# An attention layer and a triangle layer on one core: y turned by VectorE for the last batch, put-off pieces at fixed groups, bounds taken batch by batch

## The chip, the core and the metric

The kernel runs on one core of a Trainium2 chip. A core has five engines, each with an instruction queue of its own that is worked off in order: TensorE (PE in the profile; its weight loads are PEld), VectorE (DVE), ScalarE (ACT), GpSimd (POOL) and SyncE (SP), which here only starts DMAs. Engines wait for one another through semaphores. The metric is the device time of one execution in microseconds; lower is better.

## The reference

The input x is 4 batches of 64 x 64 positions with 256 channels, so 4096 tokens per batch, in float32. Two layers follow one another.

Layer 0 is self-attention over the 4096 tokens of a batch, with 32 channels for queries and keys and 128 for values:

```python
s = jnp.einsum('bqd,bkd->bqk', g, f)
beta = jax.nn.softmax(s, axis=-1)
o = jnp.einsum('bqk,bkd->bqd', beta, v)
o = o @ Wo + bo
return x + o.reshape(b, h, w, c)
```

Layer 1 takes its result y as a 64 x 64 map and does triangle attention with 8 heads of 32 channels, then a projection, a residual with y, a layer norm, a two-layer MLP and a second layer norm:

```python
att = jax.nn.softmax(scores, axis=2)
out = jnp.einsum('biljh,bilhd,bljhd->bijhd', att, v1, v2)
attn_out = out.reshape(B, N, N, E) @ Wo
h = _layer_norm(x_in + attn_out, ln_agg_g, ln_agg_b)
mlp = jax.nn.relu(h @ W1 + b1) @ W2 + b2
return _layer_norm(mlp + h, ln_out_g, ln_out_b)
```

## The kernel before

The whole order of instructions is written out by hand; nothing is reordered inside `tc.manual_schedule()`. `run` goes through the four batches, and for each through layer 0 (`layer0`) and layer 1 (`first_layer1` or `next_layer1`). At the end, `rest.alone` does what is left of batch 3's tokens.

**Layer 0** (lines 498 to 844). A batch has 8 blocks of 512 queries (`NQB`), and each block has 8 groups (k = 0 to 7) of four chunks of 128 keys: 64 groups, counted by g. In group g TensorE computes the scores of group g+1 (`score`, L552) and the products with the values of group g (`values`, L579), alternating. ScalarE takes the exponential of the scores in two halves into a tile `e` (L564, tag k8, two buffers); VectorE adds `e` to the running sum `esum` (L584, L586). In group 7 VectorE adds the four quarters and splits the sum into two parts, `part` (L589 to L596, tag hid, one buffer). The work on a finished block is spread over the groups of the next one by the list `parts`: `norm` (den on TensorE, L604; then the reciprocal, L608, and oT, L610, on VectorE) and `bounds` in group 0, `output` in group 1 (y on TensorE, L631, to which VectorE adds the bias and the input, L632; y is stored to DRAM from SP, L635), and the projections to q, k, v1 and v2 (L646, L678) in groups 2 to 7, each with a copy on ScalarE into a tile `st` (three buffers) and a store from SP.

**Layer 1** (lines 848 to 1039 and 1491 to 1610) has 32 steps of products on VectorE and GpSimd (`product`, L1007) and sums of them on TensorE (`accumulate`, L1017). Word lists (ORDER, ORDER_LAST) set the order of one period, which is two steps in batches 1 to 3. `store` writes the result to DRAM.

**Tokens** (class `Tokens`, line 1044): what comes after the triangle product, in 16 pieces of 256 tokens per batch, tt = 16 b + t. The pieces of a batch run beside the layers of the next one; those of batch 3 run beside its own layer 1 (48 and 49, in part) and in `alone`. For a piece, `load` fetches the triangle result A and the piece of y; `heads` (L1120) projects A and adds y in the same PSUM accumulation. y lies in DRAM with channels first, so it has to be turned, and this is done on TensorE by a matmul against the identity, two for each half of a piece (L1125). `stats` and `roots`/`polish` make the layer norm's factors; `affine_a` applies them; `turn`, `hidden`, `rectify` and `outputs` are the MLP.

For batches 0 and 1, the last layer norm is put off: the raw sums go to DRAM, and are taken up in layer 0 of batches 2 and 3, as 16 put-off pieces. One such piece has six steps: `recall` (a DMA of 512 KB from SP into a tile `hz`, tag R, three buffers), `settle` (three two-input operations and the statistics on VectorE, L1073 to L1075, L1136, L1137), `rooted` (two small operations on ScalarE), `polished` (four small ones on VectorE, L1175 to L1178), `scaled` (two on ScalarE, L1197) and `finish` (two on GpSimd, L1287 and L1288, and a store from SP). Lines 760 to 763 set when: piece i is recalled in group 3 i, and its steps follow 3, 4, 5, 6 and 7 groups later, whatever the place of that group in its block.

**The bounds.** The sums of all softmax rows are kept in one tile `dens` for all batches (L618, L932), and two reductions at the very end (L1635, L1636) take their least and greatest value; if one is out of bounds, the kernel runs again in a safe form. These lines lie outside the manual schedule, and the compiler has set the reductions between the last products of layer 1.

SP's queue holds nearly all loads and stores in order. A DMA whose data or buffer isn't ready holds up all that stand behind it.

Of the kernel before, what the change touches and what calls it, by code (L numbers as in the profile page):

```python
# [10 lines left out]
F32 = mybir.dt.float32  # L11
# [4 lines left out]
ALU = mybir.AluOpType  # L16
AX = mybir.AxisListType

P = 128
C = 256  # L20
# [54 lines left out]
def attention_then_triangle_kernel(  # L75
# [29 lines left out]
    def ctile(shape, name):  # L105
        return const.tile(shape, F32, tag=name, name=name)
# [97 lines left out]

    dens = ctile([P, NB, 256 + 16], "dens")

# [235 lines left out]
    class Late:  # L446
# [4 lines left out]

        def load(self, q):
            self.y = []
            for cc, tag in enumerate(("A", "yc")):
                t = work.tile([P, 512], F32, tag=tag, name="yb", bufs=1)
                nc.sync.dma_start(out=t, in_=self.io["y"][ts(cc, P), ts(q, 512)])
                self.y.append(t)
            self.used = 0
# [39 lines left out]
    def layer0(b, F, safe, rest, ahead):  # L498
# [6 lines left out]
        io["q"] = dram.tile([C, 2, N, 32], F32, tag="q", name="q")  # L505
        io["v2"] = dram.tile([N, C, N], F32, tag="v2", name="v2d")
        io["v1"] = dram.tile([T, C], F32, tag="v1", name="v1d")
        L = Layer1(b, io, safe)


# [103 lines left out]
        def bounds(qb):  # L614
            for j, (t, op) in enumerate(ends.pop(qb)):
                if not safe:
                    c0 = 256 + 2 * qb + j
                    nc.vector.tensor_reduce(dens[:, b, c0 : c0 + 1], t, AX.X, op)  # L618

# [4 lines left out]
        def output(qb):  # L626
            col = ts(qb, QB)
            o = oT.pop(qb)
            for cc in range(2):
                y_ps = pb("y")  # L630
                nc.tensor.matmul(y_ps, wo0_sb[:, 0, ts(cc, P)], o, start=True, stop=True)  # L631
                nc.vector.scalar_tensor_tensor(  # L632
                    y(qb, cc), y_ps, bo_sb[:, cc : cc + 1], yT[cc][:, col], ALU.add, ALU.add
                )
                nc.sync.dma_start(out=io["y"][ts(cc, P), col], in_=y(qb, cc))  # L635


        def staged(st):
# [89 lines left out]
        if late:  # L728
            parts[3] = [lambda qb: proj(qb, "k", 0)]
            parts[4] = [lambda qb: proj(qb, "v2", 0)]  # L730
            parts[5] = [proj1_half]
            parts[6] = [lambda qb: proj(qb, "q", 1)]
            parts[7] = [lambda qb: proj(qb, "k", 1)]
        last = NQB - 1
        for r in range(4):
            score(0, r)
        for g in range(8 * NQB):
            qb, k = divmod(g, 8)
            if b == 0 and not safe:
                for load in later[3 * g : 3 * g + 3]:  # L740
                    load()
                if g == 6:
                    fold_bias()
                if g == 20:
                    add_b2()
            if safe and k == 0 and qb + 1 < NQB:
                mx, todo = pieces(qb + 1)
                for qc, t in todo:
                    max_piece(qc, t, mx)
                row[qb + 1] = max_row(mx)  # L750
            values(g, g + 1 < 8 * NQB)

            if qb > 0 and not (qb == last and k >= 6 + late):
                for part in parts[k]:
                    part(qb - 1)
            if late and g % 2 == 0 and 0 <= g // 2 - 2 < ahead.n:
                ahead.bring(g // 2 - 2)
            if late and g % 2 == 1 and 0 <= g // 2 - 3 < ahead.n:
                ahead.turn(g // 2 - 3)
            if b > 1:  # L760
                for do, late in ((rest.finish, 7), (rest.scaled, 6), (rest.polished, 5), (rest.rooted, 4), (rest.settle, 3), (rest.recall, 0)):
                    if (g - late) % 3 == 0 and 0 <= g - late < 3 * NP:
                        do(NP * (b - 2) + (g - late) // 3)
            if qb == last and k == 3:
                L.fetch_v1(0)
                L.fetch_v1(1)
            if qb == last and k == 5:
                if b > 0:
                    rest.load(NP * (b - 1))
                L.fetch_qk(0, True)  # L770
# [18 lines left out]
        if old:  # L789
            rest.stats_a(t0)  # L790
            rest.roots(0, 2)
            rest.polish(0, 2, nc.gpsimd)
        bounds(last)
        proj(last, "v2", 0, None, stage[1][:, 0, :], nc.scalar)
        L.fetch_v2(0, 1)
        mps = {}
# [53 lines left out]
    class Layer1:  # L850
        def __init__(self, b, io, safe):
            self.b, self.io, self.safe = b, io, safe

            self.aT = dram.tile([C, 2, N // 2, N], F32, tag="aT", name="aT")
            io["a"] = self.aT
            self.S, self.v2, self.qk, self.v1, self.att, self.ao = {}, {}, {}, {}, {}, {}
            self.R, self.begun, self.acc, self.rec, self.e = {}, {}, {}, {}, {}

# [60 lines left out]
        def sums(self, step):  # L921
            pair, ig = divmod(step, NIG)
            rows = self.S[pair][:, ts(ig, IG), :]
            if self.safe:
                nmx = small.tile([P, IG], F32, tag="mxl", name="mxl")
                nc.vector.tensor_reduce(nmx, rows, AX.X, ALU.max, negate=True)
                den = small.tile([P, IG], F32, tag="den", name="den")
                for i in range(IG):
                    nc.scalar.activation(rows[:, i, :], rows[:, i, :], AF.Exp, bias=nmx[:, i : i + 1])
            else:  # L930
                den = dens[:, self.b, ts(step, IG)]
            nc.vector.tensor_reduce(den, rows, AX.X, ALU.add)  # L932
            rec = small.tile([P, IG], F32, tag="rd", name="rd")
            nc.vector.reciprocal(rec, den)  # L934
            self.rec[step] = (rows, rec)
# [105 lines left out]

    class Tokens:
        def __init__(self):
            self.ios = []
            self.A, self.htp = {}, {}
            self.h, self.hT, self.hT2, self.hid, self.z, self.zp, self.hps = {}, {}, {}, {}, {}, {}, {}
            self.mv = self.rs = None
            self.raw, self.both, self.settled = {}, {}, {}  # L1050
# [44 lines left out]
        def load(self, tt, far=False):  # L1095
            b, t = divmod(tt, NP)
            if b >= len(self.ios):
                return
            io = self.ios[b]
            if far:  # L1100

                tag = ("v2", "S", "qk")[t % 3]
                both = big.tile([P, 2, 2, 256], F32, tag=tag, name="A", bufs=4 if tag == "v2" else 2)
                A, yc = both[:, 0].rearrange("p c (i j) -> p c i j", j=N), both[:, 1]
            else:
                A = work.tile([P, 2, 4, N], F32, tag="A", name="A", bufs=1)
                yc = work.tile([P, 2, 256], F32, tag="yc", name="yc", bufs=1)
            for c in range(2):
                for o in range(2):
                    nc.sync.dma_start(out=A[:, c, o : 4 : 2, :], in_=io["a"][ts(c, P), o, ts(t, 2), :])  # L1110
            nc.sync.dma_start(out=yc, in_=io["y"][:, ts(t, 256)].rearrange("(c p) t -> p c t", p=P))
            self.A[tt] = A, yc

        def heads(self, tt, n, psum=pb, new=None):
            if n == 0 if new is None else new:
                self.hps[tt] = psum("hp").rearrange("p (n c) -> p n c", n=2)
            hp = self.hps[tt]
            A, yc = self.A[tt]
            for cc in range(2):
                nc.tensor.matmul(  # L1120
                    hp[:, n, :], A[:, cc, ts(n, 2), :].rearrange("p i j -> p (i j)"), wo1_sb[:, cc, :],
                    start=(cc == 0), stop=False,
                )
            for cc in range(2):
                nc.tensor.matmul(  # L1125
                    hp[:, n, ts(cc, P)], yc[:, cc, ts(n, P)], ident, start=False, stop=(cc == 1),
                    is_transpose=True,
                )


        def stats(self, src, k, ns=range(2)):
# [5 lines left out]
                nc.vector.bn_aggr(self.mv[:, k + n, :], st)  # L1137

        def stats_a(self, tt):
            self.stats(self.hps[tt], 0)  # L1140

        def stats_o(self, tt):
# [291 lines left out]
    def first_layer1(L, ahead, F):  # L1434
# [27 lines left out]
                ahead.load(s + 2)  # L1462

        for period in range(NSTEP // 4 + 3):
            for word, late in words_of(ORDER0):
                i, last = period - late, int(word[-1])
                if word[0:2] == "sp":
# [23 lines left out]
    def next_layer1(b, L, rest, ahead, F):  # L1491
# [32 lines left out]
        def of_piece(word, q):  # L1524
# [8 lines left out]
                        load(q + 1)  # L1533
            elif word == "sa" and first:
                moments(q - 1)
                if own:
                    rest.stats(rest.hps[tt], 0)
                else:
# [51 lines left out]
        step_word, scores, take_scores = step_words(L, fetched, was_stored, spread)  # L1590
        mps[1] = {}
        for period in range(NP + 4):
            for word, late in words_of(ORDER_LAST if own else ORDER):
                i = period - late
                if own and i == 0 and word in ("A05", "A04"):
# [35 lines left out]


    lim = small.tile([P, 2], F32, tag="lim", name="lim", bufs=1)
    flat = dens.rearrange("p b n -> p (b n)")
    nc.vector.tensor_reduce(lim[:, 0:1], flat, AX.X, ALU.min)  # L1635
    nc.vector.tensor_reduce(lim[:, 1:2], flat, AX.X, ALU.max)  # L1636
    nc.vector.tensor_scalar(lim[:, 0:1], lim[:, 0:1], 1e-25, None, ALU.is_ge)
    nc.vector.tensor_scalar(lim[:, 1:2], lim[:, 1:2], 1e25, None, ALU.is_le)
    cnt = pb("cnt")
# [39 lines left out]
```

## Time and profile before

| | |
|---|---|
| median of 3 runs | 3628.52 us (3628.36 to 3633.21) |
| the profiled execution | 3633.17 us, its span 3631.4 us |
| mean granted TensorE clock | 0.994 |
| TensorE busy | 3522.3 us, 97% |
| VectorE busy | 2823.5 us, 78% |
| ScalarE busy | 1923.8 us, 53% |
| GpSimd busy | 1779.2 us, 49% |
| layer 0 of batches 0 to 3, from its first to its last value matmul | 45 to 411, 874 to 1262, 1734 to 2124, 2597 to 2987 us |
| tail (`alone`), in steady pieces | about 3480 to 3610 us |

Times in the profile count from the span's start. A line of a timeline gives the start, the time from the start of the first to the end of the last instruction merged into it, the engine, the line in the kernel, the operation, the tile written and the tiles read, and in brackets the idle time before it with what ended it. Matmuls overlap, so the length of one is more than its share of the array's time; the distance of starts tells that. A list of groups gives for each kind of instruction its count, its busy time, the mean length in ns and the idle time before it. A list of waits gives who waited for whom: total, times, longest. A table of stretches gives for each engine the busy time, then the granted TensorE clock, the share of time that the DMA engines were busy, and GB/s.

### The profile page before, as it was taken

To read this page: it belongs to the slowest core of one execution; us is meant where nothing else is said; L and a number is where in the kernel's file an instruction comes from. 1 tells how busy PE (TensorE), PEld (TensorE's weight loads), DVE (VectorE), ACT (ScalarE), POOL (GpSimd) and SP (SyncE) were. 2 spreads that over 40 slices of the span, in tenths; PEclk is the share of its full clock that TensorE was granted. 3 is DMA by queue.
4 is the path that set the end of the run, shared out by engine and by line. 5 is a ranking of instruction groups with operands and counts; after the bars stand their busy time and mean duration, and the time that the engine had idled before them with its cause. 6 is when DMAs were issued, how large, how long until landed. Compare 5 with 4: busy or idle time off the path is not lost.

```text
span 3631.4 us, 58644 instructions
## 1 busy us (share of the span) xinstructions
PE 3522.3 (97%) x22282; PEld 1895.3 (52%) x22282; DVE 2823.5 (78%) x2558; ACT 1923.8 (53%) x4221; POOL 1779.2 (49%) x904
## 2 busy tenths in 40 slices
PE   9999999988999999999999999999899999999998
PEld 6555444434555555554455555554455555555477
DVE  4777499996555569999777549999877756999976
ACT  3444455544444366665444446666444436777655
POOL 5000099995000068889211018889611106999920
PEclk9999999999999999999999999999999999999999
DMA  9544555455111354425423254343622235441221
GB/s 174 135 131 127 136 151 137 122 134 136 47 52 52 82 145 108 101 68 107 110 91 95 67 146 109 89 104 76 132 87 95 80 93 134 92 96 46 68 68 55
DMA packets 492594, 370.15 MB, mean 102 GB/s; under 512 B 303184, under 2 KB 434000, under 8 KB 483472
## 3 DMA queue, kind: packets, MB, share of 16 engines
q1 hardware_dynamic: 443264, 339.36, 34.8%
q0 software_dynamic: 36160, 19.94, 5.3%
q10 hardware_dynamic: 12880, 7.01, 0.7%
q8 instruction: 178, 2.92, 0.4%
q14 instruction: 112, 0.92, 0.1%
HBM read 205.73 MB, written 160.43 MB: 101 GB/s over the span
## 4 chain that ended last, share of the span: by engine, by line
PE 67%; POOL 8%; DVE 6%; issue 4%; ACT 1%; DMA 1%; SPq 0%; ACTq 0%; POOLq 0%; DVEq 0%
PE o L579 16%; PE acc L1017 16%; POOL Rp L1007 7%; PE proj L646 6%; PE mp L1253 5%; PE zp L1273 5%; PE s L552 4%; PE sp L905 3%; PE hp L1120 3%; DVE R L1007 2%; PE v1p L678 2%; PE att L959 1%; PE y L631 1%; DVE rec L608 1%; PE htp L1220 1%
## 5 line engine op out<-in xcount | busy, mean ns | idle before, releaser
L1007 POOL TENSOR_TENSOR Rp<-attP,v 128x2048 f32<-128x2048 f32 x328 | 1491.4, 4579 | 409.7 <-ACT attP L967 367.0
L1007 DVE TENSOR_TENSOR R<-att,v 128x2048 f32<-128x2048 f32 x696 | 1546.1, 2279 | 68.6 <-PE acc L1017 49.9
L579 PE MATMUL o<-e,v 128*128 128x512 f32 x2048 | 1043.9, 593 | 0.0
L586 DVE TENSOR_TENSOR esum<-esum,e 128x2048 f32<-128x2048 f32 x224 | 518.8, 2316 | 398.4 <-ACT e L564 395.9
L564 ACT ACTIVATE e<-s 128x1024 f32<-128x1024 f32 x512 | 522.3, 1023 | 529.2 <-PE s L552 438.7
L552 PE MATMUL s<-gT,fT 128*128 128x512 f32 x1024 | 786.7, 770 | 8.7 <-ACT e L564 4.7
L1017 PE MATMUL acc<-R,wsel 128*32 128x512 f32 x5568 | 702.8, 599 | 26.5 <-DVE R L1007 19.6
L579 PEld LDWEIGHTS o<-e,v 128*128 128x128 f32 x2048 | 388.2, 190 | 276.8 <-issue 234.0
L1027 ACT COPY ao<-acc 128x1024 f32<-128x1024 f32 x256 | 256.4, 1013 | 290.4 <-PE acc L1017 205.8
L1017 PE MATMUL acc<-Rp,wsel 128*32 128x512 f32 x2624 | 344.3, 596 | 25.6 <-POOL Rp L1007 23.2
L1017 PEld LDWEIGHTS acc<-R,wsel 128*32 128x32 f32 x5568 | 155.5, 109 | 393.7 <-issue 273.9
L552 PEld LDWEIGHTS s<-gT,fT 128*128 128x128 f32 x1024 | 194.5, 190 | 244.7 <-issue 230.8
L1287 POOL TENSOR_TENSOR hz<-hz,log_bc 128x512 f32<-128x512 f32 x32 | 47.1, 1471 | 542.8 <-ACT hz L1197 474.4
L1181 POOL TENSOR_SCALAR nt<-mv 128x2 f32<-128x2 f32 (+1 forms) x49 | 9.4, 192 | 565.2 <-DVE mv L1137 560.1
L942 ACT ACTIVATE es<-S,rd 128x64 f32<-128x64 f32 x1024 | 258.3, 338 | 15.0 <-DVE rd L934 13.1
L1253 PE MATMUL mp<-hT,w 128*128 128x256 f32 x1024 | 244.4, 384 | 1.7 <-ACT hT L1225 1.7
L1273 PE MATMUL zp<-w,hid 128*128 128x256 f32 x1024 | 239.4, 384 | 0.8 <-ACT hid L1262 0.8
L1253 PEld LDWEIGHTS mp<-hT,w 128*128 128x128 f32 x1024 | 186.5, 190 | 53.0 <-ACT attP L967 12.6
L1273 PEld LDWEIGHTS zp<-w,hid 128*128 128x128 f32 x1024 | 188.0, 190 | 47.8 <-issue 14.7
L608 DVE RECIPROCAL rec<-den 128x512 f32<-128x512 f32 x32 | 107.4, 3357 | 109.7 <-PE den L604 104.4
L1017 PEld LDWEIGHTS acc<-Rp,wsel 128*32 128x32 f32 x2624 | 80.7, 110 | 214.1 <-issue 144.9
L915 ACT ACTIVATE S<-sp 128x512 f32<-128x512 f32 x128 | 131.6, 1094 | 78.0 <-PE sp L905 78.0
(192 smaller groups left out, 3688.4 us busy)
## 6 DMA issues: line engine op xcount, KB each, us to landing
v<-v2d SPq DMA_DIRECT2D x44, 512.0 KB
v1c<-v1d SPq DMA_DIRECT2D x128, 128.0 KB
aT<-ao SPq DMA_DIRECT2D x1024, 16.0 KB
A<-aT SPq DMA_DIRECT2D x256, 64.0 KB
hz<-raw SPq DMA_DIRECT2D x32, 512.0 KB
y<-yT SPq DMA_DIRECT2D x56, 256.0 KB
q<-st SPq DMA_DIRECT2D x56, 256.0 KB
k<-st SPq DMA_DIRECT2D x52, 256.0 KB
```

The lines of the kernel that those rows point to most:

```text
L552: nc.tensor.matmul(s_ps[r // 2][:, r % 2, :], fT[tt][:, ts(r * 4 + n, P)], gT[qb // 4][:, ts(qb % 4, QB)], start=True, stop=not safe,)
L564: nc.scalar.activation(e[g][:, 2 * j : 2 * j + 2, :], s_ps[j], AF.Exp)
L579: nc.tensor.matmul(o_ps[qb], F.v[tt][:, r * 4 + n, :], es[:, r, :], start=(k == 0 and r == 0), stop=(k == 7 and r == 3),)
L586: nc.vector.tensor_tensor(esum[qb], esum[qb], es, ALU.add)
L608: nc.vector.reciprocal(rec, den)
L646: nc.tensor.matmul(ps, w[:, cc, rows], y(qb, cc), start=(cc == 0), stop=(cc == 1))
L942: nc.scalar.mul(e[:, i, :], rows[:, i, :], rec[:, i : i + 1])
L1007: eng.tensor_tensor(R, src.unsqueeze(1).to_broadcast([P, D, N]), v2[h], ALU.mult)
L1017: nc.tensor.matmul(acc[32 * c : 32 * c + 32, n % 2, :], w[:, n, c, 16 * h : 16 * h + 32], R[:, ts(c, 8), :].rearrange("p d j -> p (d j)"), ...
L1027: nc.scalar.copy(self.ao[step][:, ts(np, 2)].rearrange("p k d j -> p k (d j)"), self.acc[step][np])
L1253: nc.tensor.matmul(self.mp[:, fc % 2, :], w1_sb[:, cc, ts(fc, P)], self.hT[tt][:, cc, :], start=(cc == 0), stop=(cc == 1),)
L1273: nc.tensor.matmul(zp[:, n, :], self.hid[tt][:, fc, ts(n, P)], w2_sb[:, fc, :], start=(fc == 0), stop=(fc == 3 and tt not in self.hT2),)
```

## The change

There are three parts.

1. For the last batch (`turned_ahead(b)`), y is turned by VectorE in layer 0: `turn_y` does eight 128 x 128 transposes (in blocks of 32 x 32) per block in group 5 of the next block, into a tile of tag hid, and stores it from SP with four DMAs to a new DRAM tensor `yt`, tokens first, in runs of 256 bytes. For the last block this is done after the loop, into a tile of tag k8, and the stores are issued in period 1 of layer 1 (`L.owed`). `heads` leaves out the turning matmuls for this batch; `load` fetches from `yt`, and `add_y` adds the piece to PSUM on VectorE, ahead of the statistics.
2. The put-off pieces no longer come every third group. Blocks 0 and 1 take up three pieces each, blocks 2 to 6 two each, and block 7 none. Piece t of a block is recalled in group t, settled in group 2 + t + t//2, and so on; none of the steps of a piece passes its block's group 7.
3. `dens` holds one batch. `limits(b - 1)` takes its least and greatest value in group 1 of the next batch's layer 0, and `limits(NB - 1)` at the end.

```diff
-    dens = ctile([P, NB, 256 + 16], "dens")
+    dens = ctile([P, 256 + 16], "dens")
+    lims = ctile([P, 2, NB], "lims")
+    def limits(b):
+        for j, op in enumerate((ALU.min, ALU.max)):
+            nc.vector.tensor_reduce(lims[:, j, b : b + 1], dens, AX.X, op)
...
+        def turn_y(qb, **where):
+            t = work.tile([P, 16, 2, 32], F32, name="yr", **where)
+            for cc in range(2):
+                rows = y(qb, cc).rearrange("p (k t) -> p k t", t=32)
+                for k in range(4):
+                    nc.vector.transpose(t[:, ts(k, 4), cc, :], rows[:, ts(k, 4), :])
+            def kept():
+                for r in range(4):
+                    nc.sync.dma_start(
+                        out=io["yt"][ts(qb, QB), ts(r, 64)].rearrange("(k t) c -> t k c", t=32),
+                        in_=t[ts(r, 32)].rearrange("t k h c -> t k (h c)"),
+                    )
+            return kept
...
+        if turned_ahead(b):
+            parts[5].append(lambda qb: turn_y(qb, tag="hid", bufs=1)())
...
-                for do, late in ((rest.finish, 7), (rest.scaled, 6), (rest.polished, 5), (rest.rooted, 4), (rest.settle, 3), (rest.recall, 0)):
-                    if (g - late) % 3 == 0 and 0 <= g - late < 3 * NP:
-                        do(NP * (b - 2) + (g - late) // 3)
+                first = 3 * qb if qb < 2 else 2 + 2 * qb
+                for t in range(3 if qb < 2 else 2 if qb < last else 0):
+                    for do, at in (
+                        (rest.recall, t), (rest.settle, 2 + t + t // 2), (rest.rooted, 3 + t + t // 2),
+                        (rest.polished, 4 + t + t // 2), (rest.scaled, 5 + t + t // 2), (rest.finish, 7),
+                    ):
+                        if k == min(at, 7):
+                            do(NP * (b - 2) + first + t)
+            if g == 1 and b > 0 and not safe:
+                limits(b - 1)
...
         bounds(last)
+        if turned_ahead(b):
+            L.owed = turn_y(last, tag="k8")
...
+    def turned_ahead(b):
+        return b == NB - 1
...
+            src = io["yt"][ts(t, 256)] if turned_ahead(b) else io["y"][:, ts(t, 256)]
+            nc.sync.dma_start(out=yt, in_=src.rearrange("(n p) c -> p n c", p=P))
...
-                    start=(cc == 0), stop=False,
-                )
-            for cc in range(2):
-                nc.tensor.matmul(
-                    hp[:, n, ts(cc, P)], yc[:, cc, ts(n, P)], ident, start=False, stop=(cc == 1),
-                    is_transpose=True,
-                )
+                    start=(cc == 0), stop=(cc == 1 and turned_ahead(tt // NP)),
+                )
+            if not turned_ahead(tt // NP):
+                for cc in range(2):
+                    nc.tensor.matmul(
+                        hp[:, n, ts(cc, P)], self.yt[tt][:, cc, ts(n, P)], ident, start=False, stop=(cc == 1),
+                        is_transpose=True,
+                    )
+
+        def add_y(self, tt):
+            hp, yt = self.hps[tt], self.yt.pop(tt)
+            if not turned_ahead(tt // NP):
+                return
+            for n in range(2):
+                own = hp[:, n, :].rearrange("p (h r c) -> p h r c", h=2, r=4)
+                nc.vector.tensor_tensor(own, own, yt[:, n, :].rearrange("p (r h c) -> p h r c", h=2, r=4), ALU.add)
...
         def stats_a(self, tt):
+            self.add_y(tt)
             self.stats(self.hps[tt], 0)
...
+            if period == 1:
+                L.owed()
...
-    flat = dens.rearrange("p b n -> p (b n)")
-    nc.vector.tensor_reduce(lim[:, 0:1], flat, AX.X, ALU.min)
-    nc.vector.tensor_reduce(lim[:, 1:2], flat, AX.X, ALU.max)
+    limits(NB - 1)
+    nc.vector.tensor_reduce(lim[:, 0:1], lims[:, 0], AX.X, ALU.min)
+    nc.vector.tensor_reduce(lim[:, 1:2], lims[:, 1], AX.X, ALU.max)
```

## The prediction

> **What bounds the kernel now.** I read the page's first part, then TensorE's list of waits batch by batch, then the timelines of the blocks in which a wait stands, then the groups of the operations that the change adds or removes.
>
> ```profile
> span 3631.4 us, 58644 instructions
> PE 3522.3 (97%) x22282; PEld 1895.3 (52%) x22282; DVE 2823.5 (78%) x2558; ACT 1923.8 (53%) x4221; POOL 1779.2 (49%) x904
> ```
>
> TensorE runs for 97% of the span, so time can only come from its waits or from work taken off it. Its waits in layer 0 of batch 2 (window 1733 to 2130):
>
> ```profile
> PE proj L646 <- DVE yT L632: 1.9, 2, 1.0
> PE y L631 <- DVE oT L610: 0.3, 1, 0.3
> ```
>
> Group starts on the timeline of TensorE show what these are: a block of eight groups takes 50.8 us, but 52.0 in blocks 3 and 6, where put-off piece work (settle) falls on group 0 behind the softmax division, and 51.6 in block 1. Over undisturbed blocks that is 1.2 + 1.2 + 0.8 = 3.2 us, in batches 2 and 3 alike: 6.4 us in all. Batch 1, without put-off pieces, has none of it.
>
> Block 0 of batch 2 on VectorE (start, length):
>
> ```profile
> 1748.47 2.29 DVE L586 TENSOR_TENSOR esum<-esum,e 128x2048 f32<-128x2048 f32 x1 [2.06 <-ACT e L564]
> 1750.68 0.69 DVE L1073 TENSOR_TENSOR hz<-hz,lag_bc 128x512 f32<-128x512 f32 x1
> ...
> 1753.94 2.26 DVE L586 TENSOR_TENSOR esum<-esum,e 128x2048 f32<-128x2048 f32 x1
> ...
> 1766.98 3.33 DVE L586 TENSOR_TENSOR esum<-esum,e 128x2048 f32<-128x2048 f32 x1
> 1770.35 2.18 DVE L589 TENSOR_TENSOR esum<-esum 128x1024 f32<-128x1024 f32 x1
> ```
>
> A settle takes 3.26 us (1750.68 to 1753.94). The last two lines are 1.0 and 0.9 us longer than usual (2.29, 1.23); POOL is then in a finish whose second operation is stretched from 1.28:
>
> ```profile
> 1768.24 3.20 POOL L1288 TENSOR_TENSOR hz<-hz,lob_bc 128x512 f32<-128x512 f32 x1
> ```
>
> So each collision of a finish with VectorE's two-input sums costs VectorE about 1 us. What a settle waits for, on the DMA queue and in the stretches (last two numbers: DMA share, GB/s):
>
> ```profile
> 1738.35 0.43 SPq L417 DMA_DIRECT2D yT<-ahx  x1
> 1738.87 1.89 SPq L1068 DMA_DIRECT2D hz<-raw  x3
> ```
> ```profile
> 1742.00:1746.00 4.00, 4.00 (x12) 2.00 (x11) 2.34 (x2) 1.78 (x2) 0.00 (x0) 1.00 1.05 444
> 1746.00:1748.00 2.00, 2.00 (x8) 1.04 (x6) 0.42 (x1) 0.85 (x2) 0.00 (x0) 1.00 0.88 369
> 1748.00:1750.00 2.00, 2.00 (x8) 1.13 (x6) 1.53 (x1) 0.85 (x2) 0.00 (x0) 1.00 1.02 416
> ```
>
> The three recalls stand behind 3 MB of v and yT. Adding up GB/s from 1738, 3.67 MB (v, yT, first recall) are through at 1748.3; with a lagging engine I take 1749.6. The same sum in batch 3 gives 2611.6.
>
> The groups of the turning:
>
> ```profile
> L1125 PE MATMUL hp<-ident,yc 128*128 128x128 f32 x200 | 38.2, 273 | 0.0
> L356 DVE STREAM_TRANSPOSE xr<-xr 128x128 f32<-128x128 f32 x192 | 48.6, 388 | 0.0
> L1343 DVE TENSOR_TENSOR z<-zp,z 128x256 f32<-128x256 f32 x2 | 0.8, 404 | 0.0
> L1635 DVE TENSOR_REDUCE lim<-dens 128x1 f32<-128x1088 f32 x1 | 1.3, 1271 | 0.0
> ```
>
> And one piece of the tail on TensorE, from one hp to the next:
>
> ```profile
> 3502.93 1.03 PE L1120 MATMUL hp<-wo,A 128*128 128x256 f32 x4
> 3503.80 0.38 PE L1125 MATMUL hp<-ident,A 128*128 128x128 f32 x2
> 3504.01 1.03 PE L1120 MATMUL hp<-wo,A 128*128 128x256 f32 x4
> 3504.88 0.38 PE L1125 MATMUL hp<-ident,A 128*128 128x128 f32 x2
> 3505.10 0.60 PE L1220 MATMUL htp<-ident,h 128*128 128x128 f32 x4
> ```
>
> Starts count here: two turning matmuls hold the array from 3503.80 to 3504.01, 0.21 us. Pieces follow each other every 9.51 us without a gap.
>
> **The change part by part.** All sums are differences against the profiled execution, which took 3633.17 us (span 3631.4), 4.65 us over the median of 3628.52; I apply them to the median.
>
> *Turning matmuls gone, sums added (tail).* Four per piece: 0.43 us, so TensorE needs 9.08 per piece. VectorE gets two 128x256 sums from PSUM, 0.42 each by L1343's row. Its loop per piece runs from the first hp statistics (3543.35) to the last small operation (3551.70): 8.35 us, with two waits of 0.60 for ScalarE in it; then 1.17 us idle until hp. With the sums it needs 9.2, more than TensorE's 9.08, so VectorE sets the pace: 0.31 saved over 11 steady pieces, -3.5 us. Ends: TensorE keeps the pace over 14 pieces, -6.0; a sum costs as much as the 128x512 one of L1145 (0.68), loop 9.7, +2. I take -3.5, since L1343 has the right width. Pieces 48 and 49 run beside layer 1, where VectorE is busy 95%: +0.3 (0 to +0.8).
>
> *turn_y.* Eight transposes of 0.388 per block, 3.1 us on VectorE in group 5, which lasts 7.8 us and in which VectorE otherwise has one 2.3 us esum: hidden by the projections of that group. In block 1 a settle and a polish stand there too, 9.6 us; the 1.8 left over is made up in group 6. For the last block it stands in an idle stretch of VectorE (2998.9 to 3019.7); its four stores are issued in period 1 of layer 1, behind SP's loads for the start, and the k8 buffer they read is next wanted by ao of step 1, a period of 27 us later: 0. Without this cover it would cost 3.1 a block. The four stores of a block (0.55 each on SP) come behind the q store (2723.68 in block 2 of batch 3), so until 2726; behind them SP has the k store of 2729.8 and, in block 7, the loads of A, needed at 2989.5 and now there some 2 us before: 0 (to +1). Their buffer is shared with part, written at 2731.2. The nearest row, the v2 store of half the bytes in 256-byte rows, issued at 2735.81, is through by 2739.2; twice that ends near 2730, and den needs part only near 2739. Cost 0. [...]
>
> *Fixed groups.* Gone: the settles of group 0, and block 1's old wait: -6.4. In blocks 2 to 6 settles fall in groups 2 and 3 (VectorE 5.8 us in groups of 6.1 and 7.8): no wait follows. In block 0 groups last 4.35 and now hold three settles. Batch 2, group 2 from 1744.0: esum(2) ends 1746.4, settle waits for the recall (queued behind it: esum(3), then ScalarE's exponentials, which need e's buffers, then TensorE). Then without a pause: settle 1752.9, esum(3) 1755.1, settle 1758.4, esum(4) 1760.6, polish 1761.3, esum(5) 1763.5, polish 1764.2, settle 1767.5, esum(6) 1769.7, esum(7) 1771.9, half sums and part 1775.2, polish 1775.9; with one collision for each of two finishes, 1777.9. Scaled for the third piece stands on ScalarE in group 7 behind that polish: 1779.0; the exponential behind it ends 1780.1, and the score matmul that needs its buffer was due at 1774.6. Wait: 5.5 us. In batch 3 the recall is 0.7 earlier relative to its group: 4.8. Together 10.3, so +3.9 net. Ends: no collision and no late recall, about 0; two collisions for each finish, 14.3, and 2 more if block 1's third piece does the same at its end (by the same walk its exponential has 0.2 us to spare). SP holds the third store of block 0 until that finish ends, with recall and the y stores behind it; they are needed two groups later.
>
> *The clock.* TensorE's granted clock was 0.50 for 3.4 us after idle gaps of 2.55 us (at 414) and 2.46 (at 1718), but stayed at 1.00 after 2.46 at 2580. The new wait falls in two pieces of about 2.5 us (before den and before the score): I take one drop in two batches, 3.4 us at half speed, +1.7 (0 to +6.8). [...]
>
> *Bounds by batch.* limits adds two reductions of 272 columns (0.4 each) at group 1, where VectorE idles 4.4 us: 0. At the end the two 1.27 us reductions (3449.7, 3451.3) stand between products, and TensorE then waits 1.34 for R; they shrink by 1.7 in all: -1.0 (-1.3 to 0).
>
> Sum: -3.5 + 0.3 + 3.9 + 1.7 - 1.0 = +1.4: 3629.9 us.
>
> **The rivals.** *Faster:* VectorE's backlog never reaches TensorE and TensorE keeps the tail's pace: -6.4 - 6.0 - 1.0 = -13.4, 3615. For it: in block 3 a finish collided in group 7 and block 4 shows no wait. Against: the settles alone are 9.8 us in six groups of 4.35 that already hold 2.2 each.
> *Slower:* the same backlog at its upper end, 16.3 us in both batches, with clock drops of 6.8 us: +9.9 + 6.8 - 3.5 - 0.7 = +12.5, 3641. It decides once wait and drops pass 18 us for both batches. For it: VectorE would have no idle time from 1749.6 on. Against: a finish cost 2 us only where sums followed one another closely.
> *part waits for the stores of turned y:* from 5.5 us of lateness on each us costs six blocks 1 us; 2 more make +12, 3642. Against: the v2 store's 3.4 us.
> *The tail gains nothing* because the sums bound it: 3633.4, still no change.
>
> **How the numbers follow.** Forecast 0.50, tail without gain 0.10, faster 0.15, backlog 0.20, stores 0.05. About 0.2% (7.3 us) is what a measurement can tell from no change: faster 0.15, same 0.60, slower 0.25. Most of the chance lies within; the forecast's own range is 3622 to 3636. Leaving out the outer halves of the rivals gives 3619 to 3641.
>
> **What would show it.** In layer 0 of batches 2 and 3, blocks 3 and 6 take 50.8 us and block 1 some 56; VectorE has no gap from the first settle to rec; exponentials wait for scaled. Tail pieces follow every 9.2 us, and the gap before the hp statistics is gone. No turning matmul reads the last batch's y. It is wrong if recalls land sooner, if POOL collides otherwise, or if a sum on PSUM in place costs more than 0.42.

## The result, and the profile after

The changed kernel takes 3636.01 us in the median of 20 runs (3630.58 to 3640.49), the kernel before 3632.49 us in 20 runs beside it (3624.61 to 3635.48). The ratio is 1.0014, with a 95% interval of 1.0008 to 1.0021: 2.9 to 7.6 us longer. That is clearly more than nothing, and its upper end lies at the prediction's bound for no change (0.2%, 7.3 us). The forecast of 3629.9 us was worked out on a median of three runs of before that lay 4 us lower; as a difference it was +1.4 us. The profiled execution of after took 3637.93 us, its span is 3636.1 us (before 3631.4).

The first part of the page, after:

```profile
span 3636.1 us, 58663 instructions
...
PE 3521.2 (97%) x22218; PEld 1888.1 (52%) x22218; DVE 2862.1 (79%) x2662; ACT 1922.6 (53%) x4221; POOL 1770.2 (49%) x904
```

The shares say nothing: 64 matmuls fewer, 104 VectorE instructions more. The difference is read by stages: layer 0 from the start of the first value matmul (L586) to the start of the last one and its step of 0.43 us, and the tail from the last hp of layer 1's rhythm (at 3458.65 before and 3467.26 after) to the end. All are worked out from starts in the traces:

```
                        before   after   difference   predicted
layer 0, batch 1        387.6    387.3      -0.2          0
layer 0, batch 2        390.5    396.2      +5.7      +2.3 and half of the clock's 1.7
layer 0, batch 3        390.6    394.8      +4.3      +1.6 and the other half
period before the tail   27.22    27.20      0.0       -0.7 (bounds, pieces 48 and 49)
tail, entry to end      172.7    168.8      -3.9       -3.5
```

These rows add up to +5.8 us; the spans differ by 4.7, since the stretches that the table leaves out are 1.1 us shorter after (layer 0 of batch 0, for one, starts at 43.62 instead of 45.27).

**Layer 0.** TensorE's list of waits of after in batch 2, behind the ramp at the start of the batch, its first group of 5.7 us (1742 to 2129; columns: us in total, times, longest):

```profile
PE s L559 <- ACT e L571: 5.4, 4, 2.2
PE den L611 <- DVE part L603: 0.6, 1, 0.6
```

The waits of proj for yT at the starts of blocks 3 and 6 are gone, as predicted; these two took their place. The timeline of TensorE puts all five of them into block 0 (1732.5 to 1772.7) and the first group of block 1:

```profile
1755.79 0.50 PE L559 MATMUL s<-gT,fT 128*128 128x512 f32 x1 [0.20 <-ACT e L571]
...
1761.22 0.50 PE L559 MATMUL s<-gT,fT 128*128 128x512 f32 x1 [0.82 <-ACT e L571]
...
1772.32 0.50 PE L559 MATMUL s<-gT,fT 128*128 128x512 f32 x1 [2.14 <-ACT e L571]
...
1777.79 0.49 PE L611 MATMUL den<-part,ones_f 128*128 128x512 f32 x1 [0.62 <-DVE part L603]
...
1780.48 0.50 PE L559 MATMUL s<-gT,fT 128*128 128x512 f32 x1 [2.20 <-ACT e L571]
```

In group starts: block 0 takes 40.12 us instead of 36.15 and block 1 takes 55.76, its first two groups 8.16 and 7.75 where batch 1, without pieces, has 4.82 and 6.16. In the second of them the granted clock is 0.50 for 3.4 us (from 1781.03). Blocks 2 to 6, with two pieces in each, take 50.82. Each of these stalls costs some 0.27 us more than the wait that the profile prints: group 4 is 0.47 longer for a wait of 0.20, group 5 1.08 for 0.82, group 7 2.41 for 2.14.

VectorE in block 0 of batch 2, after (start, length; the 5.53 are two sums in a row, 2.26 and 3.17):

```profile
1749.09 0.69 DVE L1112 TENSOR_TENSOR hz<-hz,lag_bc 128x512 f32<-128x512 f32 x1 [4.01 <-DMA hz<-raw]
...
1763.21 1.22 DVE L1227 SCALAR_TENSOR_TENSOR rn<-nt,rs 128x2 f32<-128x2 f32 x1
1764.46 0.16 DVE L1228 SCALAR_TENSOR_TENSOR rn<-mv,rn 128x2 f32<-128x2 f32 x1
1764.54 1.77 DVE L1112 TENSOR_TENSOR hz<-hz,lag_bc 128x512 f32<-128x512 f32 x1
...
1768.89 5.53 DVE L593 TENSOR_TENSOR esum<-esum,e 128x2048 f32<-128x2048 f32 x2
...
1778.24 0.16 DVE L1228 SCALAR_TENSOR_TENSOR rn<-mv,rn 128x2 f32<-128x2 f32 x1
```

And GpSimd in the same stretch:

```profile
1763.14 1.27 POOL L1337 TENSOR_TENSOR hz<-hz,log_bc 128x512 f32<-128x512 f32 x1 [31.60 <-ACT hz L1247]
1764.49 1.27 POOL L1338 TENSOR_TENSOR hz<-hz,lob_bc 128x512 f32<-128x512 f32 x1
1767.09 1.80 POOL L1337 TENSOR_TENSOR hz<-hz,log_bc 128x512 f32<-128x512 f32 x1 [1.33 <-ACT hz L1247]
1768.98 3.30 POOL L1338 TENSOR_TENSOR hz<-hz,lob_bc 128x512 f32<-128x512 f32 x1
```

VectorE idles 4.01 us for the recall, then has no gap until the reciprocal behind 1778.24. Three of GpSimd's four operations hit one of its instructions and lengthen it: L1227 by 1.06, L1112 by 1.08, the second sum by 0.9, 3.0 us in all. The third piece's polish ends at 1778.40, and ScalarE shows who was waiting for it:

```profile
1778.43 1.09 ACT L1247 ACTIVATE hz<-hz,rn 128x256 f32<-128x256 f32 x2 [5.25 <-DVE rn L1228]
1779.43 1.92 ACT L571 ACTIVATE e<-s 128x1024 f32<-128x1024 f32 x2
```

ScalarE, in order, idles 5.25 us for the scaled step of this piece; the exponentials behind it, and with them the score matmul of 1780.48, come late.

**Tail.** The adding of y costs what its row was taken for (groups of after; behind the bar the busy time and the mean ns of one):

```profile
L1177 DVE TENSOR_TENSOR hp<-hp,A 128x256 f32<-128x256 f32 x28 | 12.1, 432 | 3.5 <-PE hp L1160 3.0
...
L651 DVE STREAM_TRANSPOSE yr<-yT 128x128 f32<-128x128 f32 x56 | 11.6, 273 | 0.0
...
L213 DVE TENSOR_REDUCE lims<-dens 128x1 f32<-128x272 f32 x8 | 3.2, 427 | 0.0
```

The first four steady pieces follow each other by 9.07 us, the other seven by 9.19. Before, VectorE still waited for hp in each piece:

```profile
3543.35 0.43 DVE L1136 BATCH_NORM_STATS2 st<-hp 128x6 f32<-128x256 f32 x1 [1.17 <-PE hp L1125]
```

VectorE in one of the later ones, after, from one wait for ScalarE to the next:

```profile
3557.47 0.16 DVE L1225 SCALAR_TENSOR_TENSOR nt<-mv,rs 128x2 f32<-128x2 f32 x1 [0.60 <-ACT rs L1215]
...
3558.13 0.90 DVE L1177 TENSOR_TENSOR hp<-hp,A 128x256 f32<-128x256 f32 x2
3559.07 0.43 DVE L1185 BATCH_NORM_STATS2 st<-hp 128x6 f32<-128x256 f32 x1
...
3560.85 0.16 DVE L1225 SCALAR_TENSOR_TENSOR nt<-mv,rs 128x2 f32<-128x2 f32 x1 [0.60 <-ACT rs L1215]
...
3566.66 0.16 DVE L1225 SCALAR_TENSOR_TENSOR nt<-mv,rs 128x2 f32<-128x2 f32 x1 [0.60 <-ACT rs L1215]
```

The 1.17 us of idling ahead of the hp statistics is gone, L1177 stands directly behind the polish, and the loop of 3557.47 to 3566.66 is 9.19 us: VectorE sets the pace.

In the period before the tail, TensorE before (first line) and after:

```profile
3454.86 1.92 PE L1017 MATMUL acc<-R,wsel 128*32 128x512 f32 x16 [1.34 <-DVE R L1007]
```
```profile
3462.53 1.92 PE L1052 MATMUL acc<-R,wsel 128*32 128x512 f32 x16 [0.81 <-DVE R L1042]
...
3467.26 1.99 PE L1160 MATMUL hp<-wo,A 128*128 128x256 f32 x8 [1.09 <-ACT z L1247]
```

### The profile page after: what moved, and what is told of

It reads as the page before. It is cut to its first block, busy times and chain, and to the rows that moved or that the text cites. A ratio compares the mean times of both kernels' runs of the same rounds, so it can differ in the third digit from the quotient of the medians.

```text
span 3636.1 us, 58663 instructions
## 1 busy us (share of the span) xinstructions
PE 3521.2 (97%) x22218; PEld 1888.1 (52%) x22218; DVE 2862.1 (79%) x2662; ACT 1922.6 (53%) x4221; POOL 1770.2 (49%) x904
## 4 chain that ended last, share of the span: by engine, by line
PE 64%; DVE 9%; POOL 6%; issue 4%; ACT 2%; DMA 2%; SPq 0%; ACTq 0%; DVEq 0%; POOLq 0%
PE acc L1052 17%; PE o L586 16%; PE proj L669 6%; POOL Rp L1042 6%; PE zp L1323 4%; PE s L559 4%; PE mp L1303 4%; DVE R L1042 4%; PE sp L940 3%; PE v1p L701 2%; PE hp L1160 2%; PE y L638 1%; PE att L994 1%; DVE esum L593 1%; DVE st L1185 1%
## 5 line engine op out<-in xcount | busy, mean ns | idle before, releaser
L586 PE MATMUL o<-e,v 128*128 128x512 f32 x2048 | 1046.9, 594 | 0.0
L586 PEld LDWEIGHTS o<-e,v 128*128 128x128 f32 x2048 | 388.7, 190 | 276.6 <-issue 233.9
```

The lines of the kernel that those rows point to most:

```text
L586: nc.tensor.matmul(o_ps[qb], F.v[tt][:, r * 4 + n, :], es[:, r, :], start=(k == 0 and r == 0), stop=(k == 7 and r == 3),)
```

## The experiments

Two theories were to be told apart: that block 0's third piece is too much for the short groups (which would make the whole loss), or that the loss comes with the turning of y or the tail. Within the first, three causes were then taken away one at a time.

**Fixed groups alone**: the kernel before with nothing but the new loop.

```diff
-                for do, late in ((rest.finish, 7), (rest.scaled, 6), (rest.polished, 5), (rest.rooted, 4), (rest.settle, 3), (rest.recall, 0)):
...
+                first = 3 * qb if qb < 2 else 2 + 2 * qb
+                for t in range(3 if qb < 2 else 2 if qb < last else 0):
...
```

> The kernel before with the fixed groups alone. Theory: layer 0 of batch 2 takes 396 us and of batch 3 some 395, as in the changed kernel, two drops of the granted clock in block 1, and the time is 9 to 11 us above the kernel before. Rival (in batch 3 it is turn_y that lengthens layer 0): batch 3 stays at 390.6 and the time is only 5 to 6 above.

Measured: 3642.11 us, ratio 1.0031 (1.0018 to 1.0043). Layer 0 takes 396.56 and 394.97 us in batches 2 and 3, with two clock drops (3.4 us at 0.50 from 1776.6 and 2643.6). Its waits in batch 3:

```profile
PE s L552 <- ACT e L564: 4.3, 2, 2.2
PE den L604 <- DVE part L596: 0.6, 1, 0.6
```

The whole loss of 10.4 us in layer 0 is the loop's, without y being turned, and batch 3 loses as much with the turning (394.84) as without it.

**Old put-off times**: the changed kernel with the loop of before.

```diff
-                first = 3 * qb if qb < 2 else 2 + 2 * qb
...
+                for do, late in ((rest.finish, 7), (rest.scaled, 6), (rest.polished, 5), (rest.rooted, 4), (rest.settle, 3), (rest.recall, 0)):
...
```

> The changed kernel with the old times of the put-off pieces (every third group), so turned y and bounds by batch alone. Theory (the backlog in block 0 of batches 2 and 3 is the whole loss): layer 0 of batches 2 and 3 is back at 390.5 us each, tail pieces still follow every 9.1 to 9.2 us, and the time is 4 to 6 us below the kernel before. Rival (turn_y or the sums cost time too): layer 0 of batch 3 above 392, or the time not below the kernel before.

Measured: 3628.78 us, ratio 0.9993 (0.9984 to 1.0002); layer 0 is back at 390.61 and 390.57, the tail's pace is 9.07 and then 9.19 as in after. Its waits in batch 2 are the old ones:

```profile
PE proj L669 <- DVE yT L639: 1.9, 2, 1.0
PE y L638 <- DVE oT L617: 0.3, 1, 0.3
```

The rest of the change gains 2.5 us by the ratio (from 5.8 gained to 0.7 lost), where 4 to 6 were expected; the traces say 3.9 of the tail. What of it is the tail's and what chance can't be told by times of this spread.

**None in block 0**: the changed kernel, with the pieces per block 0, 3, 3, 3, 3, 2, 2, 0 instead of 3, 3, 2, 2, 2, 2, 2, 0.

```diff
-                first = 3 * qb if qb < 2 else 2 + 2 * qb
-                for t in range(3 if qb < 2 else 2 if qb < last else 0):
+                n, first = (0, 3, 3, 3, 3, 2, 2, 0)[qb], (0, 0, 3, 6, 9, 12, 14, 16)[qb]
+                for t in range(n):
```

> The changed kernel with no put-off piece in block 0, three each in blocks 1 to 4 and two each in blocks 5 and 6. Theory (the short groups of block 0 and the late recall are what the three pieces do not fit into): no wait of TensorE in blocks 0 to 6, layer 0 of batches 2 and 3 at 387.5 us as in batch 1, and the time 9 to 12 us below the kernel before. Rival (three pieces in a block are too many anywhere, since the exponential behind the third scaled piece has only 0.2 us to spare): groups 0 of blocks 2 to 5 take over 5.5 us instead of 4.8, more so in batch 3, and the time is less than 6 us below the kernel before.

Measured: 3621.23 us, ratio 0.9971 (0.9960 to 0.9982): some 10.5 us below the kernel before, where 9 to 12 were expected. Layer 0 takes 387.34 and 387.42, as batch 1 without any pieces; behind the ramp TensorE has no wait in it, and the clock no drop. Three pieces in a block cost nothing where groups last 4.8 to 7.8 us. So it is block 0, whose groups last 4.35, and not the count as such.

**Tail's finish on GpSimd**: the kernel above, and in the tail the gain and bias of the piece before on GpSimd.

```diff
-                    self.finish(tt - 1, V)
+                    self.finish(tt - 1)
```

> As e3_none_in_block_0, and in the tail the last scaling and shift of a piece (finish) is done by GpSimd instead of VectorE. Theory (VectorE's loop of 9.19 us sets the tail's pace): without 1.45 us of it TensorE sets the pace at 9.07 for all pieces, and the time is 1 to 3 us below e3_none_in_block_0. Rival (collisions with GpSimd give VectorE back about 1 us for each of the two operations): the pieces stay at 9.2 or more and nothing is gained.

Measured: 3616.73 us, ratio 0.9963 (0.9950 to 0.9977), the fastest kernel of this study. Pieces follow by 9.07 us throughout, and VectorE, relieved of two operations of 0.69, waits for hp again:

```profile
3555.05 0.16 DVE L1225 SCALAR_TENSOR_TENSOR nt<-mv,rs 128x2 f32<-128x2 f32 x1 [0.60 <-ACT rs L1215]
...
3555.94 0.90 DVE L1177 TENSOR_TENSOR hp<-hp,A 128x256 f32<-128x256 f32 x2 [0.15 <-PE hp L1160]
```

So VectorE's loop did set the 9.19. GpSimd now meets VectorE here too (one L1227 takes 1.12 us instead of 0.16, at 3559.05), but that is less than was taken off. In the traces the tail is 1.6 us shorter than in the kernel without pieces in block 0 (0.8 in its steady part, 0.8 behind the last hp); 1 to 3 us were expected; the medians differ by 4.5, with intervals that overlap, and the rest of that is not explained by the edit.

**Recalls ahead of the loads**: the changed kernel, but block 0's three recalls are issued at the end of the layer 1 before, ahead of v and yT.

```diff
-                        if k == min(at, 7):
+                        if k == min(at, 7) and not (qb == 0 and do == rest.recall):
...
+            for t in range(3):
+                rest.recall(NP * (b - 1) + t)
```

> The changed kernel, but the three recalls of block 0 are issued at the end of the layer 1 before it, ahead of the loads of v and yT on SP's queue. Theory (the first settle waits for data that come behind 3 MB of loads, 3.9 us of idle VectorE): the first settle starts directly behind the second sum, at about 1745 instead of 1749, the chain without a gap that follows ends 3.5 to 4 us sooner, and the waits of block 0 and block 1 (7.3 us in batch 2, 6.0 in batch 3) fall by 3 to 4 us a batch, the clock drop perhaps with them. Layer 0 of batches 2 and 3 about 391 and 390.5 us; time 6 to 10 us below the changed kernel. Rival A (the number of settles in block 0 decides, and the early start is lost to the exponentials that VectorE then waits for): waits fall by less than 1 us. Rival B (the loads of v and yT come later instead and the first scores wait for them): the start of layer 0 loses 1 to 2 us a batch, and the gain falls to about 4 us.

Measured: 3630.69 us, ratio 0.9998 (0.9988 to 1.0007). VectorE's first settle stands directly behind the second sum, and block 0 takes 36.15 us in both batches: no wait is left in it.

```profile
1744.42 2.29 DVE L593 TENSOR_TENSOR esum<-esum,e 128x2048 f32<-128x2048 f32 x1 [0.97 <-ACT e L571]
1746.63 0.68 DVE L1112 TENSOR_TENSOR hz<-hz,lag_bc 128x512 f32<-128x512 f32 x1
```

But block 1 still takes 55.4 and 55.3, and the clock still drops in it (from 1778.1 and 2641.7). Its waits in batch 2, and ScalarE behind them:

```profile
PE s L559 <- ACT e L571: 2.2, 1, 2.2
PE den L611 <- DVE part L603: 0.3, 1, 0.3
```
```profile
1775.75 1.09 ACT L1247 ACTIVATE hz<-hz,rn 128x256 f32<-128x256 f32 x2 [5.29 <-DVE rn L1228]
```

Layer 0 falls by 4.3 and 3.1 us, against some 5.2 and 4.3 expected, and the later loads of v and yT cost nothing: from the end of one layer 0 to the start of the next it is 473.2 and 472.6 us, in the changed kernel 472.9 and 472.6. The chain on VectorE ends 4.3 us sooner after the block's start, but TensorE reaches block 1 4 us sooner too, so that the scaled step holds the exponential as long as before. The late recall makes block 0's loss, not block 1's.

**Finish without GpSimd's work**: the changed kernel, leaving out the two GpSimd operations of block 0's pieces (a gain of 1 and a bias of 0 in this case's inputs, so that this is a test and no proposal).

```diff
-            eng.tensor_tensor(z, z, log_bc.unsqueeze(1).to_broadcast([P, 2, C]), ALU.mult)
-            eng.tensor_tensor(z, z, lob_bc.unsqueeze(1).to_broadcast([P, 2, C]), ALU.add)
+            if not (eng is nc.gpsimd and b < NB - 2 and t < 3):
+                eng.tensor_tensor(z, z, log_bc.unsqueeze(1).to_broadcast([P, 2, C]), ALU.mult)
+                eng.tensor_tensor(z, z, lob_bc.unsqueeze(1).to_broadcast([P, 2, C]), ALU.add)
```

> The changed kernel, but the finish of the put-off pieces of block 0 (pieces 0 to 2 of batches 0 and 1) leaves out its two GpSimd operations (the gain log_bc and the bias lob_bc, which are 1 and 0 in this case's inputs); their stores stay. Theory (VectorE's sums are stretched while GpSimd works on a finish, 3.0 us in block 0 of batch 2): the stretched sums, 3.2 and 1.8 and 1.2 us long, return to 2.3 and 0.7 and 0.2, the third polish ends some 3 us sooner, and the waits at the end of block 0 and at the start of block 1 shrink by 2 to 4 us a batch, with the clock drop gone where a gap falls below 2 us. Layer 0 of batches 2 and 3 about 392 and 391 us; time 5 to 9 us below the changed kernel. Rival (the stretching is VectorE's own waiting for exponentials, or the recall alone is the cause): the lengths return but the waits do not, or the lengths stay; no more than 1 us.

Measured: 3629.69 us, ratio 0.9999 (0.9990 to 1.0009). The lengths return (L1112 too, 0.69):

```profile
1763.53 0.16 DVE L1227 SCALAR_TENSOR_TENSOR rn<-nt,rs 128x2 f32<-128x2 f32 x1
...
1767.08 4.66 DVE L593 TENSOR_TENSOR esum<-esum,e 128x2048 f32<-128x2048 f32 x2
```

The third polish ends at 1775.7, and layer 0 takes 391.71 and 390.52: 4.5 and 4.3 us less. The wait at the end of block 0 falls from 2.14 to nothing that the profile shows, and the clock stays at full speed (1.00 from 1771 to 1783.5 in batch 2). The wait for the exponential at the start of block 1 stays (2.19), so some 1.6 us of each gain is the clock drop, which did not follow this gap (the section on the hardware has the stretches). The other 2.8 us or so are the collisions': they were a cause, not a by-product.

**Third piece's scaled step later**: the changed kernel, but scaled and finish of the third piece of blocks 0 and 1 in group 1 of the next block.

```diff
-                        if k == min(at, 7):
+                        if k == min(at, 7) and not (t == 2 and at > 6 and do in (rest.scaled, rest.finish)):
                             do(NP * (b - 2) + first + t)
+                if 1 <= qb <= 2 and k == 1:
+                    for do in (rest.scaled, rest.finish):
+                        do(NP * (b - 2) + 3 * qb - 1)
```

> The changed kernel, but the scaled step and the finish of the third piece of blocks 0 and 1 move from group 7 to group 1 of the next block; the polish stays in group 7. Theory (VectorE's backlog sets the exponentials of group 7 back because ScalarE's scaled step stands ahead of them and waits for the late polish): the wait for the exponential at the end of block 0 (2.2 us behind 5.25 idle on ScalarE) goes, and group 0 of block 1 falls from 8.16 us to about 5.4 (4.8 undisturbed, plus the 0.6 that den waits for part); without a second gap of over 2 us the clock stays at 1.00, so group 1 of block 1 returns from 7.75 to about 6.2. Block 0 itself (40.1 and 38.8 us) does not change. Layer 0 of batches 2 and 3 about 391.5 and 390 us (changed kernel 396.2 and 394.8), time about 9 us below the changed kernel. Rival A (TensorE waits because VectorE's own sums are late, whatever ScalarE does): block 1 unchanged at 55.8, no gain. Rival B (the clock drops at the start of block 1 whatever the gap): group 0 falls, group 1 stays at 7.75; about 5.5 us below.

Measured: 3630.96 us, ratio 1.0005 (0.9995 to 1.0014). Group 0 of block 1 falls from 8.16 to 5.70 and the clock stays at full speed (1.00 from 1768 to 1784 in batch 2); block 0 is as before (40.29 and 38.92). Layer 0 loses 2.8 us a batch, not the 4.7 that the theory gave, because the next lateness in the row takes over:

```profile
PE s L559 <- ACT e L571: 3.3, 3, 2.1
PE y L638 <- DVE oT L617: 0.9, 1, 0.9
PE den L611 <- DVE part L603: 0.6, 1, 0.6
```

With the exponentials free, y waits 0.94 for the softmax division, which stands behind the same polish on VectorE, and group 1 takes 7.27, not 6.2.

The three gains of batch 2 (4.3, 4.5, 2.8) add up to 11.6 where only 8.9 was lost: the 1.6 us of the clock is in two of them, and the others overlap as well. They are not shares of one sum. Nor is each needed for the next to cost something: with the recalls early, block 1 lost nearly as much as before.

The device times say the same with less certainty. By the ratios, these three kernels lie 5.8, 5.4 and 3.3 us below the changed one, each uncertain by some 4 us, where 6 to 10, 5 to 9 and 9 were expected; layer 0 of both batches falls by 7.4, 8.8 and 5.5 in the traces, of which there is one for each kernel.

## Why the prediction was right, and where its terms were not

That there would be no change beyond 0.2% was right, though not by much: the measured 0.14% has its interval's end at 0.21%, and the forecast difference of +1.4 us lies below the interval. The mechanism held: the old waits go, new ones come with block 0's three pieces, the tail gives back some of it. The sizes, term by term:

- **Turning matmuls gone, sums added** (-3.5): -3.9 from entry to end. The 11 steady pieces give 4.0 (4 x 9.07, then 7 x 9.19; predicted 9.08 and 9.2), the entry, the three steps ahead of them, 1.0, and 1.05 is given back after the last hp. Of that 0.8 goes when VectorE is relieved (tail's finish on GpSimd), so it is mostly VectorE ending late. The prediction had neither the entry nor the end; that these two cancel is luck. The row L1343 was the right one: it says 0.40, the prediction took 0.42, and a sum took 0.43.
- **Pieces 48 and 49, and bounds** (+0.3 and -1.0): 0. TensorE's wait for R shrinks from 1.34 to 0.81 as the reductions do, but in the same period its hp matmuls then wait 1.09 for ScalarE's z, a wait that before did not have there, and the period stays at 27.2 us. This is the one stall of which the prediction did not ask what is late next.
- **turn_y** (0): 0. Layer 0 of batch 3 is no longer with it than without (fixed groups alone), and part never waits for a store. The transposes took 0.27 us, not 0.39 as in the row of L356.
- **Fixed groups** (+3.9): +6.8, that is 13.2 of new waits for 10.3. This is the step that failed in size. The walk along VectorE in block 0 took 1749.6 for the recall, where settle began at 1749.09; but batch 2 began 1.3 us earlier in this execution, so that it was 0.8 late in terms of the block. It took one collision per finish where three of four operations collided, 1 us more. And it let the lateness cost TensorE once, at the exponential of 1780; in fact TensorE had already lost 4.0 us in groups 4, 5 and 7 for earlier exponentials, each stall with 0.27 us on top of its wait. That block 1 takes 55.8 us where some 56 was said is partly luck: 3.3 us of it are waits and 1.6 the clock, where 5.5 and 4.8 of waits were meant.
- **The clock** (+1.7): +3.2, 1.6 in each batch, where one drop in two batches was taken. That a drop would come was right in kind, though the gaps it was taken from were of 2.46 and 2.55 us and none here is over 2.2 us (2.20 and 2.19). Which gaps were followed by one is told below.

The terms as measured: -3.9 + 0 + 6.8 + 3.2 = +6.1 us, beside +5.1 (2.9 to 7.6) by the ratio. Of the rivals, the faster one fell with block 0's first wait; it is now known what it needed (no piece in block 0: 3621). The slower one came near: waits and drops of both batches are 16.4 us, where 18 was its turning point. The stores of turned y delayed nothing, and the tail did gain. SP held the third store of block 0 for some 10 us (1772.3 to 1782.2), as foreseen, and the recalls behind it came in time: VectorE waited for one only once in batch 2, the first.

## What to carry to other kernels

Put-off work at fixed places should be counted per place against the shortest group it can fall into, not against the mean: three pieces a block cost 16 us over two batches in the block with groups of 4.35 us (the old order lost 6 at other places), and nothing in those of 4.8 to 7.8. When the lateness of one engine is walked along, look for every consumer on the way, and for the instruction of a third engine that waits for it in order (here a scaled step on ScalarE ahead of the exponentials). And ask of each wait that goes what is late next; in batch 2 here each of three causes, taken away alone, gave back a third to a half.

## What the runs showed of the hardware

**The granted clock changed on a grid of 3.413 us.** In the traces of before and after, all 38 records of the granted clock behind the first begin on such a grid (within 0.01 us in each execution), wherever the gap was. Cutting these two traces into its windows, from 60 to 3560 us, and adding up TensorE's idle time in each window at full clock (with the ends of matmuls as the profile models them):

```
idle in the window    windows   next window at half clock
under 1.75 us          2011        0
1.75 to 2.0 us            3        1
over 2.0 us              15       15
```

So in these two executions it was not the length of a gap that decided, but how it fell into the grid: of two gaps of 2.46 us in before, the one at 1718 was followed by half clock and the one at 2580 was not. The same wait of 2.19 us at the start of block 1, behind early recalls (three stretches of 3.40 us up to and over the drop at 1778.1; the second column is the length, then the busy time of PE; PEclk is third from the end):

```profile
1771.30:1774.70 3.40, 3.40 (x11) 1.59 (x9) 3.33 (x4) 0.00 (x0) 1.89 (x1) 1.00 0.16 57
1774.70:1778.10 3.40, 0.94 (x3) 0.48 (x3) 3.30 (x7) 2.35 (x4) 1.18 (x1) 1.00 0.06 20
1778.10:1781.50 3.40, 3.40 (x7) 1.67 (x5) 3.37 (x4) 1.53 (x2) 1.36 (x2) 0.50 0.33 96
```

and without GpSimd's work:

```profile
1773.30:1776.70 3.40, 2.30 (x7) 0.94 (x5) 3.26 (x8) 0.96 (x2) 0.00 (x0) 1.00 0.00 0
1776.70:1780.10 3.40, 2.31 (x7) 1.26 (x8) 3.40 (x2) 2.63 (x4) 0.00 (x0) 1.00 0.66 206
1780.10:1783.50 3.40, 3.40 (x10) 1.68 (x9) 3.37 (x5) 1.36 (x2) 0.00 (x0) 1.00 0.06 25
```

In the first the gap lies within one stretch, with 2.46 us idle, and the next one is at half clock; in the second it is split into two of 1.1 each, and PEclk is 1.00 in all three. That a border of that execution's grid lies at 1776.7 these stretches do not show; that it spared this gap is the author's estimate from the table. Against the span's start the grid lies 1.05 us behind a multiple of 3.413 in before and 2.68 in after, so its place against the kernel was not the same in the two. A drop of 3.4 us cost some 1.6 us here (7.75 us for group 1 of block 1, 6.16 in batch 1), and the two profiles have 8 and 12 stretches at half clock. The grid also answers what the prediction had to leave as a coin's toss, the gap of 2.46 at 2580 in the kernel before that cost nothing:

```profile
2578.10:2581.50 3.40, 2.65 (x24) 0.53 (x20) 3.40 (x2) 1.28 (x2) 3.40 (x2) 1.00 0.03 9
2581.50:2584.90 3.40, 1.69 (x16) 0.57 (x20) 3.40 (x3) 0.56 (x1) 3.40 (x2) 1.00 0.00 0
```

The gap crosses the border at 2581.5: 0.75 us of idle time lie ahead of it and 1.71 behind it, neither over 1.75. In the window of the gap at 1718 TensorE idles 2.46.

**Where a two-input operation of GpSimd and one of VectorE overlapped, the later one took longer.** At 1763.21 even a 128x2 operation of VectorE, 0.16 us elsewhere in this block, took 1.22: it ended at 1764.43, 0.02 us after GpSimd's operation of 1763.14 (1.27 long). The other way round GpSimd's operation of 1768.98 took 3.30: it ended 1.12 us after the sum of 1768.89 was through, a little less than the 1.27 that it takes alone. VectorE's statistics, with one input, were not lengthened beside GpSimd's operation of 1767.09 (0.43 and 0.40, as in the settle of 1749.09 with GpSimd idle). Batch 3 shows the same lengths (1.21, 1.77, 5.53 for the two sums). So in these blocks it was not the elements that counted (1.06 us more for 128x2, 1.08 for 128x512, 0.9 for 128x2048) but how many of GpSimd's operations met a two-input one.
